# Layer-0 centring in 64x64 blocks, a gate on the GpSimd passes over y, immediates for two bias columns, and a new written order

## The chip, the cores and the metric

The kernel runs on one core of a Trainium2 chip. The metric is device time in microseconds (us) of one execution. Three runs of the kernel before gave 2687.7 (median), 2686.57 and 2696.28 us. The profile shown here is of one more execution, which took 2688.95 us; its span, from the first to the last instruction, is 2687.2 us. Engines are named as in the profile: PE (TensorE matmul), PEld (its weight loads), DVE (VectorE), ACT (ScalarE), POOL (GpSimd), SP (SyncE, which issues nearly all DMAs here).

## The reference

The input x is 16 x 32 x 128 x 128 in float32. Two pre-norm residual layers follow each other:

```python
x = x + _L0_conv_ref(_gn(x), Wq, Wkv, Wout, bout)
x = x + _L1_conv_ref(_gn(x), pn_g, pn_b, k1_..., k2_..., k3_..., k4_...)

# _gn: normalise groups of 2 channels over all positions.
# layer 0: attention between channels (heads of 64 rows, softmax over 64 x 64), projected back.
# layer 1, on 8 x 8 windows with the 32 channels last:
y = _layernorm(wins, pn_g, pn_b)                 # over the 32 channels
a = _fastkan(y seen as (.., 8 w x 2 channels))   # k1, 16 features
d = _fastkan(y seen as (.., 8 h x 2 channels))   # k2, 16 features
e = _fastkan(y as (.., 32 channels))             # k3, 32 features
z = _fastkan(a + d + e)                          # k4, 32 features
out = z + wins

def _fastkan(x, ln_g, ln_b, ws, wb, bb):
    ln = _layernorm(x, ln_g, ln_b)
    basis = exp(-((ln[..., None] - GRID) / DENOM) ** 2)   # 8 centres
    return basis @ ws.T + silu(x) @ wb.T + bb
```

## The kernel before

**Units.** After a first stage (the Gram matrix of the rows, `gram_turn` and `gram_sum`, and the 64 x 64 softmax in `attention`), layer 0 is one 256 x 256 matrix per half of the batch (`pts`). What is left is done in 64 units: 2 halves of the batch, 16 blocks of 8 image rows, 2 halves of the 256 channel rows. A unit is 128 partitions by 1024 positions. It goes through some 13 tasks, and several units are in flight at once.

**A unit's way.** `load` brings x (once for two units). `layer0_norm` multiplies by the layer-0 matrix (L1068), evicts to `xh` with the second group norm folded in (L1078), subtracts the mean over the 32 channels with a 128 x 128 centring matrix (L1083), evicts to `xc` (L1092), squares it (L1095) and forms 1/sigma (`rsqrt_rows`). `keep` writes `xh` to a scratch tensor in HBM, and `again` reads it back later for the residual. `rows_norm` multiplies (DVE, L1130) and then passes twice over y on POOL: L1134 adds the bias `pn_b` in place, L1138 writes a copy of y with the window's rows and columns exchanged. The three kinds of fastkan are done by two passes: "a" (k1 in the upper 64 partitions, k2 in the lower, on data moved by `move`), and "b" (k3 of unit n beside k4 of unit n-2). Each pass has `norm` (centring, eviction, square, 1/sigma), `scale` (DVE, L1221, twice 1024 columns), `seed` (ACT: the first basis function, and in "a" the fifth, and the ratio R), `ladder` (DVE, L1250: each further basis function is the one before it times R, clipped), and `products` (PE: the silu part at L498, then one sum of 16 32x32 blocks for each of the 8 basis functions at L478). `pair_b` adds the results of "a" with blocks of 64 x 64 (L1400 and L1421). `result` (DVE, L1472) adds the residual and `store` writes out in 4 DMAs.

**The ladder's DVE order.** A unit takes 19 DVE instructions: 6 ladder steps of "a", 7 of "b", 4 of `scale`, L1130 and L1472. Written a1..a6 and b1..b7 for the ladder steps, sa and sb for the scales, they run in a cycle: a1, sb, sb, L1472, a2, a3, a4, a5, a6, b1, b2, L1130, b3, sa, sa, b4, b5, b6, b7.

**What sets the order.** A planner (`Flow`) plays the tasks against each other with written costs, but for the busy tasks the order on each engine is written out by hand in `ORDER` (L56 to L80): `ladder_b.2.4` is step 2 of `ladder_b` for the unit 4 behind the turn's number. Every engine then works strictly in that order. Buffers are few: two PSUM tiles Y (norms and rows), two PSUM tiles X (the sums of `products`), two `xh`, one `xc`. `products` has a hop through POOL (L1274) between its first sums and the others, and SP issues all DMAs of the units in one queue: keep 4, move 8, store 4, again 4, load 8 for two units, move_back 8, move_silu 8.

Of the kernel before, what the change touches and what calls it, by code (L numbers as in the profile page):

```python
# [19 lines left out]
P = 128  # L20
NG = 8
# [22 lines left out]
LIFT = {"a": 0.0, "b": 80 * math.log(2.0)}  # L44

# [7 lines left out]
LATE = 2  # L53

# [3 lines left out]
        "products_b.3.4 products_b.4.4 products_b.5.4 layer0_norm.0.1 products_b.6.4 products_b.7.4 norm_b.4.3 "  # L58
        "products_b.8.4 products_b.9.4 norm_b.6.3 products_b.10.4 products_b.11.4 layer0_norm.2.1 products_a.0.3 "
        "products_a.2.3 products_a.3.3 layer0_norm.5.1 products_a.4.3 products_a.5.3 norm_a.0.2 products_a.6.3 "  # L60
        "products_a.7.3 norm_b.0.2 products_a.8.3 products_a.9.3 rows_norm.0.1 norm_a.4.2 products_b.0.3 "
        "norm_a.6.2 products_b.2.3 "
    ),
    "ACT": (
        "norm_b.3.3 silus.0.3 seed_a.0.3 seed_a.1.3 seed_a.2.3 norm_b.5.3 layer0_norm.1.1 seed_a.3.3 seed_a.4.3 "
        "evict_z.0.4 seed_b.0.3 layer0_norm.3.1 layer0_norm.4.1 seed_b.1.3 layer0_norm.6.1 seed_b.2.3 norm_a.1.2 "
# [3 lines left out]
        "ladder_a.2.4 ladder_a.3.4 ladder_a.4.4 ladder_a.5.4 ladder_b.0.4 ladder_b.1.4 rows_norm.1.2 ladder_b.2.4 "  # L70
        "scale_a.0.3 scale_a.1.3 ladder_b.3.4 ladder_b.4.4 ladder_b.5.4 ladder_b.6.4 ladder_a.0.3 scale_b.0.3 "
        "scale_b.1.3 result.0.6 ladder_a.1.3 "
    ),
    "SP": (
        "keep.0.1 move.0.2 store.0.6 again.0.5 load.0.0 move_back.0.3 move_silu.0.2 "
# [176 lines left out]
def conv_preact_kernel(  # L252
# [75 lines left out]
    def column():  # L328
        used[0] += 1
        return vec[:, used[0] - 1 : used[0]]  # L330

    eps, unit, ones_n = column(), column(), column()
    nc.vector.memset(eps, EPS)
    nc.vector.memset(unit, 1.0)
    nc.vector.memset(ones_n, 1.0 / S)
    zero, lift = column(), column()
    nc.vector.memset(zero, 0.0)
    nc.vector.memset(lift, LIFT["b"])
# [29 lines left out]
    c0 = const.tile([P, 4, 32], F32, name="c0")  # L368
    TS(c0, quad.unsqueeze(2).to_broadcast([P, 4, 32]), -1.0 / 32, None, ALU.mult)
    TT(c0, c0, ident.rearrange("p (q c) -> p q c", q=4), ALU.add)  # L370
    c0m = c0.rearrange("p q c -> p (q c)")
# [94 lines left out]
    C_R2, C_XB, C_P, C_B0 = range(4)  # L466
# [34 lines left out]
    def layers():  # L501
        with ExitStack() as es:
# [31 lines left out]
            rows3 = lambda t: t.rearrange("p (h w) -> p h w", h=8)  # L534

# [210 lines left out]
            def attention(bp):  # L746
# [258 lines left out]
                STT(qp, gm, cr["k4_bb"], qp, ALU.add, ALU.mult)  # L1005
# [3 lines left out]
                TT(t, t, qp, ALU.add)  # L1009
                for q in range(KK):  # L1010
                    nc.vector.tensor_copy(l0col(bp, q, C_R2), r2[:, q : q + 1])
                    nc.vector.tensor_copy(l0col(bp, q, C_XB), t[:, q : q + 1])
                    for b in range(4):
                        nc.vector.tensor_copy(
                            l0col(bp, q, C_P)[32 * b : 32 * b + 32], p_[32 * (b ^ 1) : 32 * (b ^ 1) + 32, q : q + 1]
                        )
                ps_, = yield step("PE", 0.6, "Y")
                MM(ps_[:, 0, 0:KK], lhsT=c0m, rhs=qp, start=True, stop=True)
                yield step("DVE", 0.3)
                for q in range(KK):  # L1020
                    TS(l0col(bp, q, C_B0), ps_[:, 0, q : q + 1], -1.0, None, ALU.mult)
                give("Y")
# [6 lines left out]
            def rsqrt_rows(src, e, kind):  # L1029

                parts = e.shape[1]
                lr, ve = yield step("PE", 0.24 * parts, kind, "Y")
                for j in range(parts):
                    for c in range(4):
                        u = parts * c + j
                        MM(  # L1036
                            ve[32 * c : 32 * c + 32, 0, 0:P],
                            lhsT=e[:, j, :],
                            rhs=src[:, u * P : (u + 1) * P],
                            start=j == 0,  # L1040
                            stop=j == parts - 1,
                        )
                yield step("ACT", 0.62)
                ACT(lr, ve[:, 0, 0:P], AF.Ln, bias=eps)
                ACT(lr, lr, AF.Exp, scale=-0.5)
                give("Y")
                return lr
# [13 lines left out]
            def layer0_norm(n):  # L1061
# [19 lines left out]
                xc, yp = yield step("PE", 1.94, "xc", "Y")  # L1081
                for u in range(2):
                    MM(  # L1083
                        yp[:, u, :].rearrange("p (h w n) -> p h n w", h=4, w=8),
                        lhsT=c0m,
                        rhs=xh[:, u * 512 : (u + 1) * 512].rearrange("p (h n w) -> p h n w", h=4, w=8),
                        start=True,
                        stop=True,
                    )
                used(("xh", n), "xh", 2)  # L1090
                yield step("ACT", 1.01, lag=0.0)
                ACT(xc, flat(yp), AF.Identity, bias=l0col(bp, kk, C_B0))  # L1092
                give("Y", LAG)
                sq, = yield step("ACT", 0.96, "n")
                ACT(sq, xc, AF.Square)  # L1095
                lr = yield from rsqrt_rows(sq, e0, "lr0")
                give("n")
                put(("lr0", n), (xc, lr))
# [12 lines left out]
            def rows_norm(n):  # L1111

                yield "get", "parameters"
                xc, lr = yield "get", ("lr0", n)
# [18 lines left out]
                yield step("POOL", 1.29)  # L1133
                nc.gpsimd.tensor_scalar(y, y, unit, cr["pn_b"], ALU.mult, ALU.add)  # L1134
                turned = lambda t: t.rearrange("p w (h n) -> p h w n", h=8)
                straight = lambda t: t.rearrange("p h (w n) -> p h w n", w=8)
                yield step("POOL", 1.29)
                nc.gpsimd.tensor_scalar(turned(yy[:, :, 1, :]), straight(y), unit, zero, ALU.mult, ALU.add)  # L1138
# [86 lines left out]
            def seed(name, n, par):  # L1225
# [3 lines left out]
                for k, i in enumerate(SEEDS[name]):  # L1229
# [8 lines left out]
                    yield step("ACT", 1.9 if LIFT[name] else 1.81, lag=0.0)  # L1238
                    ACT(u, u, AF.Exp, scale=-1.0, **({"bias": lift} if LIFT[name] else {}))  # L1239
                    put(("u", name, n, i), u, LAG)  # L1240

            def ladder(name, n):

                by = yield "get", ("up", name, n)
                for i in range(NG):
                    if i in SEEDS[name]:
                        at = yield "get", ("u", name, n, i)
                        continue
                    t, = yield step("DVE", 2.21, "u", lag=0.0)
                    STT(t, by, BIG, at, ALU.min, ALU.mult)  # L1250
                    used((name, n, i - 1), "u", 2)
                    put(("u", name, n, i), t, LAG)
                    at = t
                give("R", LAG)

# [5 lines left out]
            def products(name, n, wt, also, bank, ws, silus, then, cross):  # L1261
# [14 lines left out]
                for i in range(NG):  # L1276
                    t = yield "get", ("u", name, n, i)
                    yield step("PE", 1.11, lag=0.0)
# [10 lines left out]
                    used((name, n, i), "u", 1 if i + 1 == NG or i + 1 in SEEDS[name] else 2)  # L1289
# [47 lines left out]
            def evict_z(n):  # L1337
                acc = yield "get", ("z_acc", n)
                z, = yield step("ACT", 1.01, "z")
                ACT(z, flat(acc), AF.Identity, bias=cr["k3_bb"])  # L1340
# [14 lines left out]
            def norm_b(n):  # L1355
# [5 lines left out]
                rows = lambda t, h: t[:, 4 * h : 4 * h + 4, 0, :]  # L1361
                cols = lambda t, h: t[:, 512 * h : 512 * h + 512]
                two = (y, rows) if n < N else (z, cols), (z, cols) if n >= BACK else (y, rows)
# [18 lines left out]
            def pair_b(n):  # L1382
# [8 lines left out]
                def straight(acc):  # L1391
# [3 lines left out]
                    for i in range(4):  # L1395
                        v, h = i // 2, i % 2
                        for f in range(2):
# [3 lines left out]
                                    bank(acc, 64 * (f ^ h), 64, 0, h).rearrange("p (l w) -> p l w", l=4)[  # L1401
                                        :, :, 64 * v : 64 * v + 64
                                    ],
                                    lhsT=(near if v else ident)[o, o],
                                    rhs=ar[o, 4 * h : 4 * h + 4, 0, 64 * v : 64 * v + 64],
# [7 lines left out]
                def turned(acc):  # L1413
# [3 lines left out]
                    for h in range(2):  # L1417
                        for f in range(2):
# [3 lines left out]
                                    bank(acc, 64 * (1 ^ f ^ h), 64, 0, h).rearrange("p (h w n) -> p w h n", h=4, w=8),  # L1422
                                    lhsT=(near if h else ident)[o, o],
                                    rhs=ar[o, :, 1, 64 * h : 64 * h + 64].rearrange("p w (h n) -> p w h n", h=4),
# [13 lines left out]
                def silus(o, q):  # L1438
# [5 lines left out]
                    v = mine[o, 4 * h : 4 * h + 4, 0, :] if mine is t else rows3(mine)[o, 4 * h : 4 * h + 4, :]  # L1444
                    return v.rearrange("p h (w n) -> p h w n", w=8) if k else v
# [21 lines left out]
            def result(n):  # L1467
# [3 lines left out]
                yield step("DVE", 1.2)  # L1471
                STT(xh, xh, l0col(bp, kk, C_P), flat(acc), ALU.mult, ALU.add)  # L1472
# [3 lines left out]
            def store(n):  # L1476
                bp, kk, j = units[n]
                xh = yield "get", ("result", n)
                yield step("SP", 2.6, lag=0.0)
                for b in range(4):  # L1480
                    nc.sync.dma_start(
                        out=out_rows[bp * KK + kk, b, :, :, j * RB : (j + 1) * RB],
                        in_=xh[32 * (b ^ 1) : 32 * (b ^ 1) + 32, :],
                    )
                late = fl.moved(1.4, 2.0)
                give("xh", late)

            def again(n):
# [3 lines left out]
                for b in range(4):  # L1492
                    nc.sync.dma_start(out=xh[32 * b : 32 * b + 32, :], in_=xd[32 * (b ^ 1) : 32 * (b ^ 1) + 32, :])
# [5 lines left out]
            with tc.manual_schedule(engines=IN_ORDER):  # L1499
# [23 lines left out]
                        every("keep", keep),  # L1523
                        every("layer0_norm", layer0_norm),
# [88 lines left out]
```

## Time and profile before

| what | before |
|---|---|
| three runs, median | 2687.7 us |
| the profiled execution, its time and its span | 2688.95 us, 2687.2 us |
| first DVE instruction of layer 1's rows (L1130) that a ladder step follows | 231.7 us |
| result of unit 0 and of unit 63 (start of L1472) | 381.8 us, 2671.9 us |
| usual distance between two results | 36.81 us |
| granted TensorE clock, mean | 0.987 |
| DMA: mean share of the 16 engines, 400 to 2500 us | 0.53 |

The span has three parts. Up to some 200 us the Gram matrices are summed. From 200 to some 345 us the second half's attention is solved step by step between the first units. From there to some 2540 us one unit follows the other at an even distance. The rest is the last units' end, where only "b" is left.

A row of the profile's groups reads: line, engine, operation, what it writes and reads, shapes, count, then busy time and mean length of one in ns, then the idle time of the engine before these instructions and what ended it. A row of the timeline has start, length (both us), engine and line. The length of an instruction is not its cost in a queue: the next one starts before it has ended, so costs are taken as distances between starts where the text says so.

### The profile page before, as it was taken

How to read it: one execution, taken by the hardware profiler on the slowest of the kernel's cores; microseconds unless marked ns; L12 is line 12 of the kernel's file. 1: busy time of each engine (PE TensorE's matmuls, PEld its weight loads, DVE VectorE, ACT ScalarE, POOL GpSimd, SP SyncE). 2: the span in 40 equal slices, each digit the busy share in tenths (PEclk: the TensorE clock that was granted, in tenths of full speed). 3: DMA queues.
4: the chain of work that ended last, by engine and by line, in shares of the span. 5: the costliest groups of instructions: out<-in, count | busy, mean ns of one | idle time of the engine just before them, and what ended most of it. 6: DMA issues, size and time to landing. Idle time of an engine off the chain costs nothing.

```text
span 2687.2 us, 123945 instructions
## 1 busy us (share of the span) xinstructions
PE 2553.4 (95%) x56611; PEld 1300.7 (48%) x56611; DVE 2492.0 (93%) x1637; ACT 2340.5 (87%) x1967; POOL 320.6 (12%) x431
## 2 busy tenths in 40 slices
PE   6998999999999999999999999999999999999975
PEld 6884444444444444444444444444444444444432
DVE  5755799999999999999999999999999999999987
ACT  0016699999999999999999999999999999999973
POOL 4300000111101111101111011111011111011100
PEclk9998999999999999999999999999999999999988
DMA  9752345555555555555555555545555555555421
GB/s 252 189 140 64 104 119 146 144 146 148 146 142 152 151 144 140 144 144 145 147 142 150 143 151 147 146 136 149 141 152 145 142 150 142 150 150 148 135 85 45
DMA packets 289706, 379.71 MB, mean 141 GB/s; under 512 B 42400, under 2 KB 239520, under 8 KB 289184
## 3 DMA queue, kind: packets, MB, share of 16 engines
q1 hardware_dynamic: 275968, 352.48, 47.5%
q10 hardware_dynamic: 9504, 16.85, 2.4%
q8 instruction: 446, 7.31, 1.2%
q0 software_dynamic: 3712, 2.46, 0.4%
q14 instruction: 76, 0.62, 0.1%
HBM read 103.18 MB, written 67.11 MB: 63 GB/s over the span
## 4 chain that ended last, share of the span: by engine, by line
PE 80%; DVE 7%; issue 5%; DMA 1%; ACT 1%; POOL 0%; DVEq 0%; ACTq 0%; POOLq 0%
PE X L478 41%; PE Y L1068 9%; PE Y L1204 5%; PE Y L1083 5%; PE Y L478 4%; PE Y L1036 4%; PE X L498 3%; DVE u L1250 3%; DVE yy L1130 3%; PE Y L1119 2%; PE X L1400 2%; PE X L1421 2%; PE X L733 1%; DMA xh<-xh 1%; DVE yc L1221 0%
## 5 line engine op out<-in xcount | busy, mean ns | idle before, releaser
L1250 DVE SCALAR_TENSOR_TENSOR u<-R,u 128x2048 f32<-128x2048 f32 x846 | 1923.8, 2292 | 54.2 <-PE X L478 5.9
L478 PE MATMUL X<-u,wt_a 32*32 32x512 f32 x16384 | 690.4, 600 | 31.7 <-POOL vec L1274 26.4
L478 PE MATMUL X<-u,wt_b 32*32 32x512 f32 x16896 | 608.1, 601 | 13.0 <-DVE u L1250 12.2
L478 PEld LDWEIGHTS X<-u,wt_a 32*32 32x32 f32 x16384 | 297.5, 103 | 279.1 <-issue 94.9
L1231 ACT ACTIVATE u<-yc,vec 128x2048 f32<-128x2048 f32 x194 | 387.4, 1997 | 24.8 <-DVE yc L1221 17.8
L478 PEld LDWEIGHTS X<-u,wt_b 32*32 32x32 f32 x16896 | 228.0, 103 | 289.1 <-issue 123.1
L1221 DVE TENSOR_TENSOR yc<-yc,Y 128x1024 f32<-128x1024 f32 x260 | 304.9, 1214 | 9.1 <-PE Y L1204 9.0
L1195 ACT ACTIVATE yc<-Y 128x1024 f32<-128x1024 f32 x260 | 251.0, 1018 | 24.1 <-PE Y L478 24.0
L1234 ACT ACTIVATE R<-yc,vec 128x2048 f32<-128x2048 f32 x130 | 258.5, 1988 | 0.0
L1198 ACT ACTIVATE u<-yc 128x2048 f32<-128x2048 f32 x130 | 247.5, 1904 | 2.1
L1239 ACT ACTIVATE u<-u 128x2048 f32<-128x2048 f32 x128 | 243.7, 1904 | 2.0
L1068 PE MATMUL Y<-x,pt 128*128 128x512 f32 x512 | 240.1, 612 | 2.2 <-DVE yy L1130 1.3
L1274 POOL MEMSET vec<- 128x1 f32 x130 | 12.9, 99 | 1524.4 <-PE X L498 1509.7
L1134 POOL TENSOR_SCALAR yy<-yy,vec,col_r 128x1024 f32<-128x1024 f32 x64 | 168.6, 2634 | 157.0 <-DVE yy L1130 132.4
L733 PE MATMUL X<-R 128*64 128x257 f32 (+3 forms) x2048 | 151.5, 308 | 24.0 <-DVE R L707 22.4
L1068 PEld LDWEIGHTS Y<-x,pt 128*128 128x128 f32 x512 | 93.2, 192 | 147.0 <-issue 143.0
L733 PEld LDWEIGHTS X<-R 128*64 128x64 f32 x2048 | 140.7, 140 | 38.0 <-DVE R L707 25.1
L1317 ACT ACTIVATE ad<-X,col 128x1024 f32<-128x1024 f32 x128 | 135.7, 1120 | 0.3 <-PE X L478 0.2
L1239 ACT ACTIVATE u<-u,vec 128x2048 f32<-128x2048 f32 x66 | 131.3, 1989 | 0.0
L478 PE MATMUL Y<-yy,c 32*32 32x512 f32 x1056 | 129.2, 598 | 1.2 <-DVE att L894 1.2
L1083 PE MATMUL Y<-xh,c 128*128 128x512 f32 x256 | 129.3, 628 | 1.0 <-DVE yc L1221 0.7
L1152 ACT ACTIVATE S<-yy 128x2048 f32<-128x2048 f32 x64 | 122.5, 1913 | 0.7
(224 smaller groups left out, 2825.7 us busy)
## 6 DMA issues: line engine op xcount, KB each, us to landing
xh<-xh SPq DMA_DIRECT2D x512, 128.0 KB
d<-yy SPq DMA_DIRECT2D x512, 128.0 KB
sd<-S SPq DMA_DIRECT2D x512, 128.0 KB
ad_r<-ad SPq DMA_DIRECT2D x512, 128.0 KB
x<-in_x SPq DMA_DIRECT2D x256, 128.0 KB
out<-xh SPq DMA_DIRECT2D x256, 128.0 KB
u<-in_x ACTq DMA_DIRECT2D x28, 256.0 KB
u<-in_x SPq DMA_DIRECT2D x28, 256.0 KB
```

What stands on the lines that cost most here:

```text
L478: MM(dst(to, g_), lhsT=wt[32 * g_ : 32 * g_ + 32, :], rhs=rhs(g_, to ^ cross[g_]), start=start, stop=stop,)
L733: MM(g[64 * q : 64 * q + 64, k, lo:hi], lhsT=t[:, b, at : at + 64], rhs=t[:, b, lo:hi], start=first, stop=last,)
L1068: MM(xp[:, u, :], lhsT=pts[bp][:, k, kk * P : (kk + 1) * P], rhs=xr[:, k, u * 512 : (u + 1) * 512], start=k == 0, stop=k == KK - 1,)
L1083: MM(yp[:, u, :].rearrange("p (h w n) -> p h n w", h=4, w=8), lhsT=c0m, rhs=xh[:, u * 512 : (u + 1) * 512].rearrange("p (h n w) -> p h n w ...
L1134: nc.gpsimd.tensor_scalar(y, y, unit, cr["pn_b"], ALU.mult, ALU.add)
L1195: ACT(v[:, i * RB : (i + 1) * RB], flat(yt[i]), AF.Identity)
L1198: ACT(sq, v, AF.Square)
L1221: TT(v[:, o], v[:, o], flat(rb[i]), ALU.mult)
L1231: ACT(u, v, AF.Square, bias=bqs[k])
L1234: ACT(up, v, AF.Exp, bias=bp_, scale=2.0)
L1239: ACT(u, u, AF.Exp, scale=-1.0, **({"bias": lift} if LIFT[name] else {}))
L1250: STT(t, by, BIG, at, ALU.min, ALU.mult)
```

## The change

1. **Centring in blocks.** The two 128x128 matmuls of `layer0_norm` become four of 64x64, which lie in the four quadrants of the array. Their weights `c0w` also divide by the residual's factor, which is prepared in `attention`. So `xc` no longer needs a bias column, and `result` no longer multiplies. The columns of a PSUM tile are now halves of windows (index u) instead of upper and lower image rows, and everything that reads or adds there follows: `norm_b`, `pair_b`, `evict_z`.
2. **The square reads PSUM; the copy is a task of its own.** ACT squares `yp` directly, and `centre` copies it to `xc` later, so that `yp` stays in PSUM for longer.
3. **result, store, again.** `result` adds in two halves of 512 columns, each with its own bias column; `store` has 8 DMAs of 512 columns; `again` has 4 DMAs of 64 partitions by 512 columns.
4. **POOL.** The pass that turns the window now comes first and adds the bias on the way; the pass in place comes second. From unit 3 on the first pass waits for a ladder step (b3) of two units back.
5. **Immediates.** `eps` in the logarithm and `LIFT` in the seed are numbers instead of columns.
6. **A new ORDER.** On DVE the cycle of a unit is the one shown above, with two instructions in L1472's place. On PE, `rsqrt_rows` of `norm_b` comes two basis functions earlier, the 1/sigma rows of `rows_norm` (L1119) come after `norm_a`'s and not before, and the sums of the layer-0 squares come before the first basis function of "a". On SP, again and load come before store.

`HALVES` is empty, so `assist` and the branches that ask for it do nothing.

```diff
+EARLY = 3
+GATE = ("b", 3)
...
 def layer0_norm(n):
...
-                xc, yp = yield step("PE", 1.94, "xc", "Y")
+                yp, = yield step("PE", 1.02, "Y")
                 for u in range(2):
-                    MM(
-                        yp[:, u, :].rearrange("p (h w n) -> p h n w", h=4, w=8),
-                        lhsT=c0m,
-                        rhs=xh[:, u * 512 : (u + 1) * 512].rearrange("p (h n w) -> p h n w", h=4, w=8),
...
+                    for f in range(2):
+                        o = slice(64 * f, 64 * f + 64)
+                        MM(
+                            yp[64 * (f ^ u) : 64 * (f ^ u) + 64, u, :].rearrange("p (h w m) -> p h m w", h=8, w=8),
+                            lhsT=c0w[o, bp, kk, :],
+                            rhs=xh[o].rearrange("p (h u m w) -> p u h m w", h=8, u=2, m=8)[:, u],
...
-                ACT(xc, flat(yp), AF.Identity, bias=l0col(bp, kk, C_B0))
-                give("Y", LAG)
-                sq, = yield step("ACT", 0.96, "n")
-                ACT(sq, xc, AF.Square)
+                put(("yp", n), yp, LAG)
+                sq, = yield step("ACT", 0.94, "n")
+                ACT(windows(sq), chunks(yp), AF.Square)
...
+            def centre(n):
+                yp = yield "get", ("yp", n)
+                xc, = yield step("ACT", 1.01, "xc")
+                nc.scalar.copy(windows(xc), chunks(yp))
...
 def rows_norm(n):
...
-                yield step("POOL", 1.29)
-                nc.gpsimd.tensor_scalar(y, y, unit, cr["pn_b"], ALU.mult, ALU.add)
...
-                nc.gpsimd.tensor_scalar(turned(yy[:, :, 1, :]), straight(y), unit, zero, ALU.mult, ALU.add)
+                if n >= EARLY:
+                    before = yield "get", ("laid", n - 2)
+                yield step("POOL", 1.22, lag=0.0)
+                add = nc.gpsimd.tensor_scalar(turned(yy[:, :, 1, :]), straight(y), unit, cr["pn_b"], ALU.mult, ALU.add)
+                if n >= EARLY:
+                    after([add], [before])
+                yield step("POOL", 1.22)
+                nc.gpsimd.tensor_scalar(y, y, unit, cr["pn_b"], ALU.mult, ALU.add)
...
-                ACT(lr, ve[:, 0, 0:P], AF.Ln, bias=eps)
+                ACT(lr, ve[:, 0, 0:P], AF.Ln, bias=EPS)
...
-                    ACT(u, u, AF.Exp, scale=-1.0, **({"bias": lift} if LIFT[name] else {}))
+                    ACT(u, u, AF.Exp, scale=-1.0, bias=LIFT[name])
...
+                        laid = STT(t, by, BIG, at, ALU.min, ALU.mult)
+                        if (name, i) == GATE:
+                            put(("laid", n), laid, LAG)
...
-                ACT(z, flat(acc), AF.Identity, bias=cr["k3_bb"])
+                ACT(windows(z), chunks(acc), AF.Identity, bias=cr["k3_bb"])
...
 def result(n):
-                yield step("DVE", 1.2)
-                STT(xh, xh, l0col(bp, kk, C_P), flat(acc), ALU.mult, ALU.add)
+                yield step("DVE", 1.3)
+                for h, c in enumerate((C_B, C_BX)):
+                    o = slice(512 * h, 512 * h + 512)
+                    STT(xh[:, o], xh[:, o], l0col(bp, kk, c), acc[:, h, :], ALU.add, ALU.add)
...
 def store(n):
-                for b in range(4):
+                for i in range(8):
+                    b, h = i // 2, i % 2
+                    at = j * RB + HALF * h
                     nc.sync.dma_start(
-                        out=out_rows[bp * KK + kk, b, :, :, j * RB : (j + 1) * RB],
-                        in_=xh[32 * (b ^ 1) : 32 * (b ^ 1) + 32, :],
+                        out=out_rows[bp * KK + kk, b, :, :, at : at + HALF],
+                        in_=xh[32 * (b ^ 2 * h) : 32 * (b ^ 2 * h) + 32, HALF * h : HALF * h + HALF],
                     )
```

## The prediction

> **What bounds the kernel now.** I read the page first: busy time, then the chain of work that ended last.
>
> ```profile
> PE 2553.4 (95%) x56611; PEld 1300.7 (48%) x56611; DVE 2492.0 (93%) x1637; ACT 2340.5 (87%) x1967; POOL 320.6 (12%) x431
> ...
> PE 80%; DVE 7%; issue 5%; DMA 1%; ACT 1%; POOL 0%; DVEq 0%; ACTq 0%; POOLq 0%
> ```
>
> Three engines are nearly full, and the chain names PE. But a chain only goes back to whatever ended last at each step; with three full engines it can stay on one that has spare time. So I asked next, for the even stretch from 400 to 2500 us, what DVE does and what it waited for.
>
> ```profile
> L1250 DVE SCALAR_TENSOR_TENSOR u<-R,u 128x2048 f32<-128x2048 f32 x741 | 1684.2, 2292 | 38.6 <-DVE u L1250 0.9 <-PE X L478 0.5
> L1221 DVE TENSOR_TENSOR yc<-yc,Y 128x1024 f32<-128x1024 f32 x228 | 267.4, 1214 | 1.6 <-PE Y L1204 1.6
> L1472 DVE SCALAR_TENSOR_TENSOR xh<-xh,l0c,X 128x1024 f32<-128x1024 f32 x57 | 72.7, 1275 | 0.0
> L1130 DVE TENSOR_TENSOR yy<-xc,Y 128x1024 f32<-128x1024 f32 x57 | 69.2, 1214 | 0.0
> ```
>
> In 2100 us DVE stood idle for 40, and only 2.1 of them ended with an event on PE (1.6 and 0.5). The rest are gaps of about 0.1 us between a ladder step and the next, which needs its result. So **DVE sets the pace**: a unit takes 36.81 us (results at 1045.17 and 1081.98) because its 19 DVE instructions take that long. PE has spare time twice per unit: in the timeline it waits 0.41 us for L1130 and about as long for POOL's hop. ACT waits 35.4 us in this stretch for L1036. What the change saves on PE or ACT is worth little unless DVE's own sequence gets shorter.
>
> **Part by part.** *Centring in blocks.* Two rows bear on it:
>
> ```profile
> L1083 PE MATMUL Y<-xh,c 128*128 128x512 f32 x256 | 129.3, 628 | 1.0 <-DVE yc L1221 0.7 <-DVE u L790 0.3
> ...
> L1421 PE MATMUL X<-ad_r,near 64*64 64x512 f32 x256 | 68.9, 614 | 0.0
> ```
>
> L1083 takes 129.3 / 64 = 2.0 us per unit. L1421 already sends four 64x64 blocks of 512 columns through the four quadrants: 1079.47 to 1080.49, or 1.02 us. So the new centring costs 1.02, and PE saves about 1 us per unit, 64 us in all. None is on the path: PE is held by L1130 and by the result, both on DVE. Were PE the bound, these 64 us would be the gain.
>
> *Other patterns of columns.* Matmuls now read or write in runs of 8 columns. Half the "b" blocks of L478 already write PSUM with a step of 8 columns, and "b" averages 601 ns against 600 for "a". The Trainium skill (SBUF — State Buffer, Door 1: The DMA port swizzle) says that any non-contiguous PSUM pattern slows matmuls significantly. It gives no figure; the row shows no such loss, so by the row the term is 0. Reads in runs of 8 are in no row: between no change and a doubling; I take no change, nearest to the runs of 64 that L1421 reads, and keep the other end as a rival.
>
> *ACT.* L1239 takes 1989 ns with a bias column and 1904 without: 0.08 us per unit saved, three logarithms about as much each, and `xc` loses its column too: some 0.4 in all. Worth nothing, as ACT waits anyhow. Writing in runs of 8 is in no row (runs of 64, L1317, cost 1120 ns against 1098 for L1340); doubled, three instructions would cost 3 us and make ACT the bound; I take 0.
>
> *result in halves.* One instruction of 1.275 us, 1.19 from start to start (1081.98 to 1083.17), becomes two of 512 columns. Nearest row: L894, 512 columns from PSUM with a column operand, 728 ns; less the overlap of 0.083, twice 0.645 is 1.29: +0.10. By half the difference between L1250's 2048 and L1472's 1024 columns (2.292 - 1.275 = 1.017, half 0.51) a half takes 0.767: +0.18. I take +0.12, nearer to L894, times 64 = **+7.7 us**, all on DVE's path; ends 0 and +0.18.
>
> *The gate.* DVE's order puts b3 right behind L1130, then two scales, then b4. Here are DVE and POOL in one unit:
>
> ```profile
> 1062.48 1.21 DVE L1130 TENSOR_TENSOR yy<-xc,Y 128x1024 f32<-128x1024 f32 x1
> 1063.62 2.28 DVE L1250 SCALAR_TENSOR_TENSOR u<-R,u 128x2048 f32<-128x2048 f32 x1
> 1065.82 2.35 DVE L1221 TENSOR_TENSOR yc<-yc,Y 128x1024 f32<-128x1024 f32 x2
> 1068.08 2.33 DVE L1250 SCALAR_TENSOR_TENSOR u<-R,u 128x2048 f32<-128x2048 f32 x1
> ```
>
> ```profile
> 1064.20 2.77 POOL L1134 TENSOR_SCALAR yy<-yy,vec,col_r 128x1024 f32<-128x1024 f32 x1 [0.39 <-DMA xh<-xh]
> 1067.07 1.20 POOL L1138 TENSOR_SCALAR yy<-yy,vec 128x1024 f32<-128x1024 f32 x1
> ```
>
> L1134 starts inside b3 and takes 2.77 instead of 1.20: it stands until b3 has read, then works beside the scales. L1138 ends at 1068.27, 0.19 after b4's start, and b4 takes 2.33 instead of 2.29. So a ladder step and a POOL pass exclude each other, whoever came first; scales and passes don't. One early step shows the larger price:
>
> ```profile
> 233.79 2.59 DVE L1250 SCALAR_TENSOR_TENSOR u<-R,u 128x2048 f32<-128x2048 f32 x1 [0.84 <-ACT u L1239]
> ```
>
> ```profile
> 233.05 1.20 POOL L1134 TENSOR_SCALAR yy<-yy,vec,col_r 128x1024 f32<-128x1024 f32 x1 [47.33 <-DVE yy L1130]
> ```
>
> Here the pass ends 0.46 after the step's start, and the step takes 0.30 more. Both cases give: cost = overlap - 0.15.
>
> Now the first pass waits until b3 has *ended* (1065.90). POOL's other waits are there today too: at 437 us L1130 ends at 437.50 and L1134 starts at 437.67, so 0.16 later. First pass 1066.06 to 1067.26, 0.10 between, second 1067.36 to 1068.56: 0.48 into b4, cost 0.33 instead of 0.04. That is +0.29 for each of the 61 units from unit 3 on, **+17.7 us**. Ends: -0.04 (b4 keeps POOL out) and +0.44 (the whole overlap). Behind the gate POOL has only its second pass and, 10 us later, the tick of L1410, so nobody else waits; y is first wanted a period later. The Trainium skill (SBUF — State Buffer, Who interferes with whom) says that a DVE instruction with two SBUF inputs and a GpSimd one that reads SBUF exclude each other for the whole instruction; it speaks against this gate. By its full overlap b4 pays 0.48 after and 0.19 before, the same difference; only the price paid today would be 11.6 us instead of 2.6.
>
> *Order, DMAs, edges.* DVE's cycle is unchanged, so are its gaps. PE's way from L1130 to the next sb carries the same work; it arrives 0.18 us early today (L1204 ends 1079.54, sb starts 1079.72), and DVE's later b4 widens that: the 1.6 us of waits for L1204 go. SP has 4 more issues of 0.7 us per unit. Per pair of units its issuing takes some 61 us of 73.6, so some 67 after, still inside; the 8 stores carry the same bytes, and again and load no longer queue behind them. If that cover went, move_back would be late for L1400. At the start (200 to 345 us, DVE idle for 48) PE's saving and one matmul less in `attention` can give some 5, the gate can take 2 or 3; I take -2. The end keeps its chain: ladder, products, result, store.
>
> Sum: 2688.95 + 7.7 + 17.7 - 1.6 - 2 = 2710.8 for the profiled execution; that one lies 1.25 over the median, so **2710** (2709.5).
>
> **Rivals.** (a) *The passes cost b4 nothing*: POOL yields, or its passes are shorter than in the rows. For: only two kinds of case show the price. Against: in nearly every unit b4 is the longer step. Then 2710 - 17.7 = 2692. (b) *PE sets the pace after all*, as the chain has it, and a PE that is early lets the written order close up: some 60 units at 36.8 us make up the even stretch, so 2688 - 60 = 2628 at full value. Against: DVE's waits, 2.1 us of 2100. (c) *Runs of 8 columns slow PE's reads*: L1400 lies between L1130 and sb; if its 1.02 doubled, it would exceed the spare time of 0.18 + 0.29 + some 0.1 (the first of L1204's blocks no longer wait) by 0.4 per unit: +25, 2735. It decides from 0.6 us on. (d) *The blocks run one after another*: then PE saves nothing and the time is the forecast's. Slower is already forecast; (a) and (b) are the ones that end not slower.
>
> **How the numbers follow.** Forecast with (d) 0.68, (a) 0.15, (b) or a much shorter start 0.09, (c) or ACT as the bound 0.08. The range runs from (a) to what the upper ends give (2688.95 + 64 x 0.18 + 61 x 0.44 - 3.6 - 1.25 = 2722) with part of (c): 2690 to 2732. About 0.5% is what a measurement of this kernel can tell from no change: 2674 to 2701. Faster 0.09, same 0.18, slower 0.73.
>
> **What would show it.** Results 37.2 us apart (0.41 more); two results of some 0.74 us; the first POOL pass 1.2 instead of 2.8 us long and beginning 0.16 after b3's end; b4 at 2.6 us; DVE still without waits for others; the centring at 1.0 us per unit, and PE and ACT with more idle time. It is wrong if results stand less than 36.8 us apart, or if DVE waits for PE, ACT or a DMA.

## The result, and the profile after

The changed kernel takes **2709.71 us** (median of 5 runs, 2708.75 to 2711.48) against 2687.7 for the kernel before (5 runs, 2686.04 to 2697.3): a ratio of 1.0071, 95% interval [1.0049, 1.0093]. The forecast was 2710, in a range of 2690 to 2732. The profiled execution took 2711.48 us, with a span of 2709.6 (before: 2688.95 and 2687.2).

The page of the kernel after, engines first (busy time, share of the span, instructions), then the chain by engine:

```profile
PE 2564.9 (95%) x57375; PEld 1311.1 (48%) x57375; DVE 2514.8 (93%) x1696; ACT 2313.5 (85%) x1967; POOL 229.9 (8%) x431
...
PE 68%; DVE 8%; DMA 7%; ACT 6%; issue 5%; SPq 5%; DVEq 0%; ACTq 0%; POOL 0%; POOLq 0%
```

DVE is busy 22.8 us longer, about as much as the span has grown (22.4); PE is busy 11.5 us longer although it has less to do (more on that under the doubled centring). The chain again names PE, and again it is no guide to the bound. DVE's groups from 400 to 2500 us are one (busy time, mean ns of one, idle time before them):

```profile
L1271 DVE SCALAR_TENSOR_TENSOR u<-R,u 128x2048 f32<-128x2048 f32 x733 | 1682.2, 2314 | 38.3 <-DVE u L1271 1.4
L1235 DVE TENSOR_TENSOR yc<-yc,Y 128x1024 f32<-128x1024 f32 x226 | 264.7, 1212 | 0.0
L1527 DVE SCALAR_TENSOR_TENSOR xh<-xh,l0c,X 128x512 f32<-128x512 f32 x114 | 79.7, 739 | 0.0
L1140 DVE TENSOR_TENSOR yy<-xc,Y 128x1024 f32<-128x1024 f32 x56 | 67.9, 1213 | 0.0
```

No wait for another engine is left. Two means have moved: a ladder step takes 2314 ns instead of 2292, and the result is two instructions of 739 ns instead of one of 1275. The timeline of DVE in one unit (start, us, line), b3 to b4:

```profile
1065.54 2.28 DVE L1271 SCALAR_TENSOR_TENSOR u<-R,u 128x2048 f32<-128x2048 f32 x1
1067.74 2.34 DVE L1235 TENSOR_TENSOR yc<-yc,Y 128x1024 f32<-128x1024 f32 x2
1070.00 2.62 DVE L1271 SCALAR_TENSOR_TENSOR u<-R,u 128x2048 f32<-128x2048 f32 x1
```

And POOL in the same unit:

```profile
1067.98 1.20 POOL L1148 TENSOR_SCALAR yy<-yy,vec,col_r 128x1024 f32<-128x1024 f32 x1 [3.00 <-DMA ad_r<-ad]
1069.28 1.20 POOL L1152 TENSOR_SCALAR yy<-yy,vec,col_r 128x1024 f32<-128x1024 f32 x1
```

b3 ends at 1067.82; the first pass begins 0.16 later and takes 1.20 where it took 2.77; the second pass ends at 1070.48, 0.48 into b4; and b4 takes 2.62. (The page puts POOL's wait down to a DMA. What POOL waited for is b3: from 400 us on the pass begins 0.16 us after b3's end in every unit.)

Where the 22.4 us of span went, from the starts of the results:

| stretch | before | after | difference |
|---|---|---|---|
| until the first result | 381.82 | 376.75 | -5.07 |
| the next 58 intervals | 2138.10 | 2159.54 | +21.44 |
| the last five intervals | 152.00 | 158.09 | +6.09 |
| behind the last result | 15.25 | 15.20 | -0.05 |

The median interval grew from 36.808 to 37.214, which over 58 intervals is +23.5; fewer intervals are 0.3 to 0.5 longer than the median (three instead of eight), which gives 2.1 back. Start and end, which the forecast had at -2 and 0, nearly cancel.

### The profile page after: what moved, and what is told of

Same layout as the page of the kernel before. It is cut to its first block, busy times and chain, and to the rows that moved or that the text cites. A ratio compares the mean times of both kernels' runs of the same rounds, so it can differ in the third digit from the quotient of the medians.

```text
span 2709.6 us, 126401 instructions
## 1 busy us (share of the span) xinstructions
PE 2564.9 (95%) x57375; PEld 1311.1 (48%) x57375; DVE 2514.8 (93%) x1696; ACT 2313.5 (85%) x1967; POOL 229.9 (8%) x431
## 4 chain that ended last, share of the span: by engine, by line
PE 68%; DVE 8%; DMA 7%; ACT 6%; issue 5%; SPq 5%; DVEq 0%; ACTq 0%; POOL 0%; POOLq 0%
PE X L481 33%; PE Y L1068 7%; PE Y L1036 5%; PE X L501 4%; PE Y L1218 4%; DVE u L1271 4%; PE Y L481 4%; PE X L738 3%; DMA out<-xh 2%; DVE yy L1140 2%; ACT z L1384 2%; PE Y L1129 2%; PE X L1444 2%; PE X L1468 2%; DMA u<-in_x 1%
## 5 line engine op out<-in xcount | busy, mean ns | idle before, releaser
L481 PE MATMUL X<-u,wt_a 32*32 32x512 f32 x16384 | 676.1, 603 | 5.6 <-DVE u L1271 4.8
L481 PE MATMUL X<-u,wt_b 32*32 32x512 f32 x16896 | 606.1, 601 | 12.2 <-DVE u L1271 11.5
L1253 ACT ACTIVATE u<-u 128x2048 f32<-128x2048 f32 x194 | 368.9, 1902 | 2.0
L1235 DVE TENSOR_TENSOR yc<-yc,Y 128x1024 f32<-128x1024 f32 x260 | 304.6, 1213 | 12.5 <-PE Y L1218 12.5
L501 PE MATMUL X<-sd,ws_a 32*32 32x512 f32 x2048 | 130.7, 605 | 22.0 <-ACT z L1384 17.0
L1218 PE MATMUL Y<-lr,back_a 32*128 32x128 f32 x2048 | 104.4, 289 | 38.8 <-DVE yy L1140 38.1
L1218 PEld LDWEIGHTS Y<-lr,back_a 32*128 32x128 f32 x2048 | 80.6, 185 | 103.2 <-ACT lr L1045 51.1
```

The costliest lines, as they stand in the source:

```text
L481: MM(dst(to, g_), lhsT=wt[32 * g_ : 32 * g_ + 32, :], rhs=rhs(g_, to ^ cross[g_]), start=start, stop=stop,)
L501: done.append(MM(dst(g_ ^ w, q), lhsT=wt[o, q // 2, :], rhs=rhs(o, q), start=start, stop=stop))
L1218: MM(rb[q // 2][:, q % 2, j * P : (j + 1) * P], lhsT=back[name][32 * q : 32 * q + 32, j, :], rhs=lr[32 * q : 32 * q + 32, :], start=True, ...
L1235: TT(v[:, o], v[:, o], flat(rb[i]), ALU.mult)
L1253: ACT(u, u, AF.Exp, scale=-1.0, bias=LIFT[name])
```

## The experiments

The theory: DVE sets the pace, the change lengthens DVE's sequence by 0.12 us (halves) and 0.29 us (b4 beside a POOL pass) per unit, and PE's saving is worth nothing. The rivals are those of the prediction. Of the lines of `ORDER` the edits below show only the part that changes. Ratios are to runs of the kernel before on the same chip, in three sets: there it took 2692.92 (the first four experiments), 2690.46 (the centring twice, SP's order in the kernel after, and both splits with a gate or in the kernel before) and 2688.67 us (the other three).

**Without the gate.** The kernel after, with the gate pushed out of the loop:

```diff
-EARLY = 3
+EARLY = 1000
```

> The changed kernel with the wait on b3 taken off the first GpSimd pass; the rest as in the change. Theory (DVE sets the pace, and the gate makes the second pass reach 0.48 us into b4): the first pass starts inside b3 again and stands, the second ends 0.2 us after b4's start, b4 takes 2.33 instead of 2.62 us, results stand 37.22 - 0.29 = 36.93 us apart, time 2709.7 - 60 x 0.29 = 2692. Rival (the loss comes from the new patterns of columns, the order or the DMAs, not from the gate): distance and time stay at 37.2 and 2710.

Measured: 2695.83 us (11 runs, 2691.37 to 2702.66), ratio 1.0011 [1.0002, 1.002]; results 36.925 us apart. POOL in one unit:

```profile
1065.14 3.11 POOL L1148 TENSOR_SCALAR yy<-yy,vec,col_r 128x1024 f32<-128x1024 f32 x1 [0.80 <-ACT u L1212]
1068.35 1.19 POOL L1152 TENSOR_SCALAR yy<-yy,vec,col_r 128x1024 f32<-128x1024 f32 x1
```

The first pass starts inside b3 again, stands until b3 is done, and both are through by 1069.54, 0.18 after b4's start at 1069.36. b4 takes 2.32. The gate costs 0.289 per unit. (The time fell by less than this pace gives: in the profile the first result came 4.6 us later than in the kernel after, at 381.33.)

**The gate alone**, put into the kernel before:

```diff
+EARLY = 3
+GATE = ("b", 3)
...
+                if n >= EARLY:
+                    before = yield "get", ("laid", n - 2)
                 yield step("POOL", 1.29)
-                nc.gpsimd.tensor_scalar(y, y, unit, cr["pn_b"], ALU.mult, ALU.add)
+                add = nc.gpsimd.tensor_scalar(y, y, unit, cr["pn_b"], ALU.mult, ALU.add)
+                if n >= EARLY:
+                    after([add], [before])
...
+                    laid = STT(t, by, BIG, at, ALU.min, ALU.mult)
+                    if (name, i) == GATE:
+                        put(("laid", n), laid, LAG)
```

> The kernel before with the wait on b3 put on its first GpSimd pass, and nothing else of the change. Theory: b4 takes 2.62 instead of 2.33 us, results 36.81 + 0.29 = 37.10 us apart, time 2687.7 + 17.5 = 2705. Rival (the gate costs nothing by itself, only in the new order): 36.81 and 2688.

Measured: 2708.48 us, ratio 1.0053 [1.0039, 1.0067]; results 37.094 apart (+0.286). DVE's b4, and POOL's second pass, in one unit:

```profile
1078.78 2.61 DVE L1256 SCALAR_TENSOR_TENSOR u<-R,u 128x2048 f32<-128x2048 f32 x1
```

```profile
1078.06 1.20 POOL L1144 TENSOR_SCALAR yy<-yy,vec 128x1024 f32<-128x1024 f32 x1
```

The pass ends at 1079.26, 0.48 into b4, and b4 is 0.33 longer than 2.285: the same collision as in the kernel after, without any of its other parts.

**The halves alone**, in the kernel before:

```diff
-                STT(xh, xh, l0col(bp, kk, C_P), flat(acc), ALU.mult, ALU.add)
+                for h in range(2):
+                    o = slice(512 * h, 512 * h + 512)
+                    STT(xh[:, o], xh[:, o], l0col(bp, kk, C_P), acc[:, h, :], ALU.mult, ALU.add)
```

> The kernel before with its result written as two instructions of 512 columns, and nothing else of the change. Theory: two steps of 0.66 us in place of one of 1.19, results 36.81 + 0.13 = 36.94 us apart, time 2687.7 + 64 x 0.13 = 2696. Rival (the split is hidden in waits that DVE has anyway): 36.81 and 2688.

Measured: 2698.68 us, ratio 1.0022 [1.0014, 1.0031]; results 36.926 apart (+0.118). DVE's result:

```profile
1087.96 1.41 DVE L1474 SCALAR_TENSOR_TENSOR xh<-xh,l0c,X 128x512 f32<-128x512 f32 x2
```

From its start to the next ladder step at 1089.28 are 1.32 us, against 1.19 before. Both parts together, 0.286 + 0.118 = 0.404, are the kernel after's 0.406.

**The centring twice.** The matmuls of L1085 issued a second time, which nearly restores PE's old load (1.95 us per unit, where the kernel before spends 1.98):

```diff
-                for u in range(2):
+                for u in (0, 1, 0, 1):
```

> The kernel after, with the matmuls of the centring (L1085) issued twice: 1.02 us of PE work more in each unit, about what the centring cost before. Theory (DVE sets the pace, so PE's saving buys nothing): results still 37.21 us apart, median 2710, DVE without waits for PE. Rival (PE sets the pace after all): 64 times 1.02 = 65 us more, results 38.2 apart, 2775, and DVE waiting about 1 us per unit for PE.

Measured: 2713.82 us (4 runs, 2710.09 to 2718.14), ratio 1.0083 [1.0065, 1.0102]; results 37.216 apart, and b4 2.62. DVE's longest groups and, behind them, PE's centring and its rows, 400 to 2500 us:

```profile
L1271 DVE SCALAR_TENSOR_TENSOR u<-R,u 128x2048 f32<-128x2048 f32 x734 | 1684.6, 2314 | 38.4 <-DVE u L1271 1.4
L1235 DVE TENSOR_TENSOR yc<-yc,Y 128x1024 f32<-128x1024 f32 x226 | 264.7, 1212 | 0.1
```

```profile
L1085 PE MATMUL Y<-xh,c0w 64*64 64x512 f32 x896 | 109.1, 602 | 0.2
L1218 PE MATMUL Y<-lr,back_a 32*128 32x128 f32 x1824 | 93.3, 289 | 12.6 <-DVE yy L1140 12.6
L501 PE MATMUL X<-sd,ws_a 32*32 32x512 f32 x1792 | 89.7, 598 | 0.0
```

In the kernel after, the same three rows are:

```profile
L501 PE MATMUL X<-sd,ws_a 32*32 32x512 f32 x1793 | 117.5, 598 | 16.6 <-ACT z L1384 15.1 <-DVE xh L1527 0.8 <-DMA d<-yy 0.3
...
L1218 PE MATMUL Y<-lr,back_a 32*128 32x128 f32 x1792 | 92.4, 289 | 34.8 <-DVE yy L1140 34.8
...
L1085 PE MATMUL Y<-xh,c0w 64*64 64x512 f32 x456 | 62.1, 614 | 0.2
```

PE works 47 us more on the centring and the pace does not move: PE sets no pace here, and its saving is worth nothing in the even stretch. The rows also show why the page's PE share did not fall. The idle time before PE's groups shrinks by 39 and the busy time of L501 by 28: spare time of PE stands partly as longer busy time of a group that waits in the middle. Doubling the work shows it; the share doesn't. One thing did move: the first result comes at 383.67 instead of 376.75. That fits a start that lives on PE's saving, but it is one profile of each, and the start varies by itself: with the halves alone, where nothing ahead of the first result is edited, it comes at 384.80 instead of 381.82.

**b4 between the scales**, without the gate:

```diff
-ladder_b.2.4 scale_a.0.3 scale_a.1.3 ladder_b.3.4
+ladder_b.2.4 scale_a.0.3 ladder_b.3.4 scale_a.1.3
```

> The changed kernel without the gate, and with the second scale of a moved one place back in DVE's order: b3, sa, b4, sa, b5 instead of b3, sa, sa, b4, b5. Theory (only DVE's own sequence counts): b5 no longer stands right behind b4, on which it depends, so b4 to the next start falls from 2.40 to 2.20 us; the second pass stands through b4 and works beside the second scale, so neither step pays for a pass (0.04). Results 36.93 - 0.19 - 0.04 = 36.70 us apart, time 2692 - 14 = 2678, under both kernels. Rival (PE or ACT sets the pace, and the second half of the scaled rows comes 2.2 us later to ACT): no gain over the kernel without the gate, 2692 or more.

Measured: 2680.22 us (5 runs, 2679.17 to 2682.98), ratio 0.995 [0.9937, 0.9962]: **faster than both kernels**. Results 36.715 apart. DVE (b3, scale, b4, scale):

```profile
1315.41 2.29 DVE L1271 SCALAR_TENSOR_TENSOR u<-R,u 128x2048 f32<-128x2048 f32 x1
1317.61 1.21 DVE L1235 TENSOR_TENSOR yc<-yc,Y 128x1024 f32<-128x1024 f32 x1
1318.74 2.29 DVE L1271 SCALAR_TENSOR_TENSOR u<-R,u 128x2048 f32<-128x2048 f32 x1
1320.94 1.21 DVE L1235 TENSOR_TENSOR yc<-yc,Y 128x1024 f32<-128x1024 f32 x1
```

POOL beside it:

```profile
1315.65 3.11 POOL L1148 TENSOR_SCALAR yy<-yy,vec,col_r 128x1024 f32<-128x1024 f32 x1 [0.68 <-DMA ad_r<-ad]
1318.86 3.23 POOL L1152 TENSOR_SCALAR yy<-yy,vec,col_r 128x1024 f32<-128x1024 f32 x1
```

Each pass now starts inside a ladder step and stands until that step is done; POOL has the time, and b4 takes 2.29. Besides, b5 no longer follows b4 directly: b4 to the next start is 2.20 instead of 2.43.

**The same split with the gate kept:**

> The kernel after, gate kept, with b4 moved between the two scales of a. The gated pass still starts 0.16 us after b3 ends, but beside it stands a scale (1.13 us from start to start), so it overlaps b4 by only some 0.23 us. Theory (the gate costs by the overlap of POOL's pass with the next ladder step, overlap less 0.15): b4 takes 2.37, results about 36.80 apart, median about 2685. Rival (the gate's wait itself, or any later pass, costs the 0.29): results about 37.0 apart, median 2697.

Measured: 2688.17 us (12 runs), ratio 0.9992 [0.9981, 1.0003]; results 36.852 apart. b4, and the first pass:

```profile
1319.73 2.45 DVE L1271 SCALAR_TENSOR_TENSOR u<-R,u 128x2048 f32<-128x2048 f32 x1
```

```profile
1318.85 1.20 POOL L1148 TENSOR_SCALAR yy<-yy,vec,col_r 128x1024 f32<-128x1024 f32 x1 [2.99 <-DMA ad_r<-ad]
```

The pass overlaps b4 by 0.32, not by the 0.23 I had put down (b4 starts 1.05 after b3's end, not 1.13), and costs 0.16. So the rule held and its input was off: 2.45 instead of 2.37. The 0.29 is no price of the wait itself, which here is the same as in the kernel after.

**The split alone, in the kernel before:**

> The kernel before with one edit: ladder step b4 moved between the two scales of a (b3, scale, b4, scale, b5). Theory (DVE sets the pace in the kernel before too; one exposed gap between dependent steps and the collision of b4 with POOL's second pass go, worth 0.21 us per unit as in the ungated variant of after): results 36.60 apart, 64 times 0.21 = 13 us less, median 2674, so faster than every variant of the change. Rival (the kernel before has only 0.18 us of spare time on PE, so DVE then waits for PE's L1204 and the change's saving on PE is what made the gain possible): results at 36.7 to 36.8, median 2681 to 2688, and DVE waits ended by PE.

Measured: 2684.56 us (12 runs, 2678.23 to 2692.59), ratio 0.9977 [0.9964, 0.999]; results 36.683 apart. The scales' group:

```profile
L1221 DVE TENSOR_TENSOR yc<-yc,Y 128x1024 f32<-128x1024 f32 x230 | 274.5, 1214 | 3.3 <-PE Y L1204 2.0
```

Of 0.21 us only 0.125 is won, and the rival's first half is right: DVE waits for PE. The idle column hides most of it, because an instruction that waits a little only loses the 0.08 us by which it used to overlap the one before. The starts show it. The first scale of b comes 2.30 us behind a1 (median) instead of 2.20, and in 56 of 57 units it starts 0.034 us after the last of PE's rows ends, as here:

```profile
1333.24 1.17 PE L1204 MATMUL Y<-lr,back_b 32*128 32x128 f32 x32
1334.44 2.35 DVE L1221 TENSOR_TENSOR yc<-yc,Y 128x1024 f32<-128x1024 f32 x2
```

In the kernel before without the split, 0.173 us lie between the two.

The rival's second half, that the change's saving on PE is what lets the split work, is not borne out. The wait that counts is PE's way from the start of L1130 (L1140 after) to the end of these rows. It takes 17.06 us (median) in the kernel before, with the halves alone and with the split alone. It takes 16.95 to 16.96 in the kernel after, without the gate, with the split, and also with the centring twice: the centring is not on this way. What differs is its beginning (the kernel before, the split without the gate, the centring twice):

```profile
1322.29 1.17 PE L1204 MATMUL Y<-lr,back_a 32*128 32x128 f32 x32 [0.41 <-DVE yy L1130]
...
1314.53 0.49 PE L1218 MATMUL Y<-lr,back_a 32*128 32x128 f32 x4
1315.54 1.16 PE L1218 MATMUL Y<-lr,back_a 32*128 32x128 f32 x28 [0.53 <-DVE yy L1140]
...
1071.87 0.49 PE L1218 MATMUL Y<-lr,back_a 32*128 32x128 f32 x4
1072.58 1.16 PE L1218 MATMUL Y<-lr,back_a 32*128 32x128 f32 x28 [0.22 <-DVE yy L1140]
```

In the changed kernel four of the 32 matmuls go ahead of the wait, and the others begin 0.05 us after DVE's instruction ends instead of 0.15. Which part of the change lets the four go ahead was not tried. It is just enough: with the split and without the gate, too, the rows end only 0.035 us before the scale, so PE has no reserve left there.

Nor is it shown that the change then pays for itself. In the even stretch the kernel before with the split is the shorter one, 36.683 against 36.715 per unit. The times point the other way, 0.9977 [0.9964, 0.999] against 0.995 [0.9937, 0.9962], with intervals that nearly touch and on different chips; in the profiles the spans are 2677.5 and 2678.9 us (the first is of one of its fastest runs, 2679.25 us).

**SP's order of before, in the kernel after**, for the 6 us at the end:

```diff
-move.0.2 again.0.5 load.0.0 store.0.6 move_back.0.3 move_silu.0.2 keep.0.0
+keep.0.1 move.0.2 store.0.6 again.0.5 load.0.0 move_back.0.3 move_silu.0.2
```

> The kernel after with one edit: SP's order of before (keep, move, store, again, load, move_back, move_silu). It asks where the unpredicted loss of about 5 us at the end comes from (intervals of 40.3 and 39.1 us where the kernel before has 36.8 and 36.6). Theory (the order of SP's issues: two repeat loads stand between the store and move_back, so move_back is late for the shift matmuls): the two intervals fall to about 37.2, pace unchanged at 37.21, median 2705. Rival (PE's new order, or its later products, makes the end longer): 40 and 39 stay, median 2710.

The reason to try it is in the chain of the kernel after near its end (start, us, what):

```profile
2548.35 8.52 DMA out<-xh
2558.74 1.65 SPq L1552
2560.43 0.60 SPq L1374
...
2565.96 0.60 SPq L1374
2566.61 2.36 DMA ad_r<-ad
...
2571.39 1.76 PE Y L1218 x32
```

A store's DMAs take 8.5 us to land; `again` (L1552) waits for that and holds SP; the issues of move_back (L1374) queue behind it; the matmuls of L1444, which read what move_back brings, and the rows of L1218 behind them come late, and a scale on DVE waits 1.9 us for them.

Measured: 2707.63 us (6 runs, 2700.23 to 2712.75), ratio 1.0057 [1.004, 1.0075], an interval that overlaps the kernel after's. Results 37.216 apart; the last five intervals sum to 154.5 instead of 158.1. The sign is the theory's, and the size two thirds of it, but in one profile. The doubled centring leaves SP's order alone, and its last five intervals sum to 154.4 all the same. So a fall of 3.6 is no more than profiles with this order differ by anyway, and the order's part in the end is not shown by this run.

**Its mirror: SP's order of after, in the kernel before.**

> The kernel before with one edit: SP's order of after. The mirror of the run that gave after the order of before. Theory (the order alone makes the end longer): results 36.81 apart, the last five intervals, 152.0 us in the kernel before, sum to 155 to 157, median 2691 to 2693. Rival (the end's loss needs the change's other parts): 152, median 2688.

Measured: 2702.36 us, ratio 1.0046 [1.0033, 1.006]. The last five intervals sum to 155.9, as expected; the time is 10 us worse than expected. The even stretch lost 6.6 us too, and the scales say where:

```profile
L1221 DVE TENSOR_TENSOR yc<-yc,Y 128x1024 f32<-128x1024 f32 x228 | 267.6, 1216 | 8.8 <-PE Y L1204 8.8
```

The median interval is unchanged (36.804), but in nine units DVE waits for PE's rows, up to 2.6 us, and single intervals reach 39.5. This order, with this kernel's stores, makes PE late now and then, and the kernel before has only some 0.14 us of spare time there (0.173 less the 0.034) to absorb it. What PE itself waited for, the trace does not name, but it shows when. Eight times in the even stretch two neighbouring, equal matmuls of L478's ladder products start over 0.5 us apart (at most 2.4; in the kernel before at most 0.43). Each time the second starts 1.25 to 1.50 us after a 16 KB transfer of the kind `instruction` has landed on queue q8, where they land 5.6 us apart (median). That points to late instructions; it was not tested. In the kernel after the rows end 0.565 us ahead of the scale instead of 0.173, and there the same order shows no wait in the even stretch.

**Both good edits together** (no gate, split, SP's order of before):

> The kernel after without the gate and with b4 between the two scales, as in the earlier run of that name, and SP's order of before. Theory (SP's order of after costs some 4 to 5 us in the last units, and nothing in the even stretch): results 36.71 apart, the last five intervals sum to about 150 us instead of 153.4, median about 2676. Rival (the end's length hangs on something else): 153 and 2680.

Measured: 2679.36 us (5 runs, 2676.84 to 2683.67), ratio 0.9966 [0.9953, 0.9978]; results 36.710 apart, the last five intervals 152.1 instead of 153.4. Both are nearer to the rival's figures (153 and 2680) than to the theory's (150 and 2676). Its time and its interval can't be told from those of the run without the SP edit.

**The result behind a2**, on top of the split:

```diff
-scale_b.0.3 scale_b.1.3 result.0.6 ladder_a.1.3 ladder_a.2.3
+scale_b.0.3 scale_b.1.3 ladder_a.1.3 result.0.6 ladder_a.2.3
```

> The kernel after without the gate and with b4 between the two scales, and besides ladder step a2 ahead of the result's two halves (scale b, scale b, a2, result, a3) instead of behind them. Theory (DVE's sequence sets the pace; one more pair of dependent steps is pulled apart, worth 0.19 us): results 36.52 apart, median 2668. Rival (PE or ACT waits for the result, which comes 2.2 us later, and the loop closes through them): results at 36.72 or more, median 2680 or more, with DVE waiting for PE.

Measured: 2810.64 us, ratio 1.0459 [1.0439, 1.0479]. A clear miss. Most intervals are 37.79 or 39.33. PE's waits in the even stretch (total, times, longest), and DVE's ladder group:

```profile
PE X L501 <- DVE xh L1527: 86.9, 54, 1.9
```

```profile
L1271 DVE SCALAR_TENSOR_TENSOR u<-R,u 128x2048 f32<-128x2048 f32 x702 | 1597.8, 2289 | 132.4 <-PE X L481 101.9 <-ACT lr L1044 2.1 <-DVE u L1271 0.5
```

L501 writes X, and waits until the result has read it. Moved 2.2 us back it holds PE, and DVE then waits for PE's products, 101.9 us. The ladder steps are as short as hoped (2289); the loop closes elsewhere. With the split alone PE does not wait for the result at all, and in the kernel after 0.8 us in 2100: an edge that costs nothing can still be the next one to bind. The hope itself was too high as well: a2 and a3 stand 2.32 us apart with the split alone, not 2.39, so at most 0.12 us was to be won. The granted clock is lower in this run (0.96 to 0.98 in the even stretch), so how the loss divides between the waits and slower matmuls is open.

## Why the prediction was right

- *DVE sets the pace.* Shown: DVE has no waits for other engines after; the centring twice leaves 37.216. (The prediction says that PE is held by L1130 and by the result. The waits of the kernel before name L1130, 22.9 us, and POOL's hop L1274, 24.3 us; none is on the result.)
- *Halves, +7.7.* Shown: 0.118 x 64 = 7.6. The value was a choice between 0.10 and 0.18, and it came out.
- *Gate, +17.7.* Shown both ways: 0.286 x 61 = 17.4 by adding it, 0.289 per unit by taking it away. The rule "overlap less 0.15", drawn from two cases, held at three more: 0.48 costs 0.33 (in the kernel after and with the gate alone) and 0.32 costs 0.16. In all profiles a ladder step that begins while a pass runs pays its overlap less 0.14 to 0.15, up to the largest overlap, 1.0 us; overlaps of 0.02 cost nothing. The Trainium skill (SBUF — State Buffer, Who interferes with whom) has DVE and GpSimd exclude each other for the whole instruction. By that the three prices would be 0.48, 0.48 and 0.32; the measurement is about 0.15 less each time.
- *Waits for L1204, -1.6.* They are gone (0.0 in L1235's row), and the long intervals fell by 2.1. The spare time before the scale of b, put at 0.18 + 0.29 + some 0.1, measures 0.565 (median).
- *Start, -2: mis-sized, -5.07.* I gave PE's saving 5 and took 2 or 3 off for the gate. With the saving undone the first result comes at 383.67; the seven kernels that have it begin at 375.4 to 381.3, the five with the old centring at 381.3 to 388.0. These are single profiles, and two that share everything ahead of the first result lie 3.0 apart (381.82 and 384.80). So that the saving is worth some 5 us is likely, not shown. The gate's part can't be read from these runs: with it the first result is later in the kernel before (388.0 against 381.8) and earlier in the kernel after (376.8 against 381.3).
- *End, 0: wrong, about +5.3* (6.09 less the pace of two intervals). "The end keeps its chain" looked only at the last unit. The loss lies in the first two of the last five intervals, 40.3 and 39.1. SP's order, which I had judged by its total issue time ("still inside"), may make part of it: -3.6, +3.9 and -1.3 us in three pairs. (That total was too high, too: the issues take some 49 us per pair of units before and 57 after, not 61 and 67.) Over all profiles the last five intervals sum to 150.3 to 154.5 with the order of before (six kernels) and to 153.4 to 158.1 with that of after (seven): two groups that overlap, each wider than any of the pairs differs. So the cause of the loss stays open. PE's order changed too, and the granted clock differs there (0.95 from 2540 to 2580 us and 0.83 from 2580 to 2620, against 0.88 and 0.95 before). That start and end cancel is luck, not foresight.
- *More idle time on PE and ACT.* ACT: yes (waits of 81.5 us in the stretch instead of 35.4). PE: its idle time in the stretch rose only from 47.3 to 51.7; its spare time shows in the experiment, not in the row.
- *Rivals.* (a) is out: b4 takes 2.61 to 2.63 in 61 units. (b) is out by the doubled centring. (c) and (d) are out: L1444, which stands for L1400, has its means unchanged (402 and 376 ns). L1085 takes 614 ns on average, like the 614 of L1421 before, and 62.1 / 57 = 1.09 us per unit (put at 1.02; L1083 took 1.98). So runs of 8 columns cost nothing and the blocks run side by side. The Trainium skill (SBUF — State Buffer, Door 1: The DMA port swizzle) expects a significant loss from the pattern in PSUM; no run here shows one.

## What to carry to other kernels

When one engine has no waits, count changes on that engine's own sequence, instruction by instruction, and give work saved elsewhere the value 0. When that sequence gets shorter, ask which way on another engine its next wait closes over, and whether the saved work lies on it: here 0.10 us at one of PE's waits counted, and 0.9 us of matmuls elsewhere did not. A wait that only moves a neighbour's work to a "quiet" time should be laid on the timeline: here the passes cost 0.04 us per unit when they started inside a ladder step and stood, and 0.33 when they ran first and a step met them. Try a new order of a queue alone, and don't judge it by its total: SP's new order by itself cost the kernel before 0.5%.

## What the runs showed of the hardware

- Of a POOL pass and a ladder step that meet, the one that starts second pays. A pass that starts inside a step stands until nearly its end (1.20 becomes up to 3.25 us, and 1.07 to 1.09 of it lie behind the step's end in every profile), and the step pays nothing (2.29). A step that starts inside a pass pays its overlap less 0.15.
- A ladder step that needs the one just before it starts 2.39 to 2.40 us after it (a3 behind a2: 2.32), where another instruction in between, or a step that needs another one, lets the next start at 2.20 or 2.21. That is 0.19 us for most such pairs, and the larger part of what the split gained without the gate.
- Times go with the mean granted TensorE clock of the run, though DVE sets the pace: the kernel before on one chip took 2695.3 us (mean of 3 runs) at 0.985 and 2686.7 (4 runs) at 0.988. In the profiled runs the clock is 1.00 in the even stretch and below it only at the start (0.97 to 0.99 until 200 us, 0.88 to 0.93 from 200 to 345 us) and the end, where DVE does wait for PE. Which way the cause runs was not tried. With the result behind a2, where PE stalls in each unit, it was 0.96 to 0.98 in the even stretch as well. Whether the stalls lower the clock was not tried.
